# A list scheduler's rough clock gets other durations: a four-layer residual kernel on one core

## The chip, the core and the metric

The kernel runs on one core of a Trainium2 chip. Its time is device microseconds (us) of one execution. Five engines take part: TensorE (PE, with its weight loads listed as PEld), VectorE (DVE), ScalarE (ACT), GpSimd (POOL) and SyncE (SP), which issues most DMAs. Each engine runs its own instructions strictly in the order in which the program holds them and waits at semaphores for the others.

## The reference

`x` is [8, 512, 256], `cond` is [8, 256]. Four layers follow one another, each added to its input: `x = x + layer(x, cond)`.

```python
# L0: tanh RNN          h_t = tanh(x_t Wx + b + h_{t-1} Wh)
# L1: LSTM              i,f,o,g = split(x_t Wx + b + h_{t-1} Wh);  c_t = f c + i g;  h_t = o tanh(c_t)
# L2: hyperbolic transformer block (maps logmap0/expmap0 around each product), modulated by cond @ w_ada
xm = expmap0(layer_norm(logmap0(x)) * (1 + sc_msa) + sh_msa)
q, k, v = (to_heads(plin(xm, w, b)) for w, b in ...)          # 16 heads of 16
attn = softmax(logmap0(q) logmap0(k)^T / 4) logmap0(v)
x1 = mobius_add(x, expmap0(g_msa * logmap0(plin(from_heads(expmap0(attn)), w_o, b_o))))
ff = plin(plin(modulated(x1), w_f1, b_f1), w_f2, b_f2)        # 256 -> 1024 -> 256
out = mobius_add(x1, expmap0(g_mlp * logmap0(ff)))
# L3: mixture of experts, 4 experts of 256 -> 1024 -> 256 and a shared one
gate = softmax((means(x) @ gate_w + gate_b) * (1 + scale) + shift);  top 2, renormalised
out = sum_e w[b, e] * mask[e] * (gelu(x ew1 + eb1) ew2 + eb2) + gelu(x sw1 + sb1) sw2 + sb2
```

## The kernel before

The first half of the span (to about 1250 us) is the two recurrences with the products that feed them. The second half is the function `transformer_and_experts`, which computes the block (L2) and the experts (L3) for the eight batch elements b = 0 to 7, 512 tokens each.

**Pieces and streams.** The second half is written as Python generators, each of which emits instructions and yields where another may go on. They are put into nine streams:

- Stream 0 is the main one, which keeps TensorE full: attention(0), attention(1), attention(2), then experts(b-3) and attention(b) in turn for b = 3 to 7, and last experts(5), experts(6), experts(7). Call "a period" one experts(b-3) with the attention(b) that follows it.
- Streams 1 to 4 carry batch element b from its attention to its experts: `last_sums` and `drain` (1), `close` (2), `feed_forward` (3), `end` (4). In data order: `end` divides the attention sums (tiles `ov`, `o`), transposes (`p_oT`), multiplies with w_o (`pao`, `ao`), adds the residual (`ra_...`) and modulates (`mf_...`); `feed_forward` transposes (`p_mT`) and multiplies (`pf`, `f`, `f2`); `close` adds the second residual (`rf_...`), transposes the result into `xT` (`pyT`), makes the gate (`gs`, `pg`) and the experts' input `xf`, a copy of `xT` rounded for TensorE.
- Streams 6 to 8 prepare the heads of later elements (`heads_inputs`, `heads`: tiles `q`, `k`, `v`, `scales_...`, transposes `q_p`, `k_p`, copies `q_t`, `k_t`) and transpose and store finished elements (`pout`). Streams 3 to 7 can be held back for a while (`HELD`).

In an attention each slot has a score product `sc` (64x128 by 64x512), ACT's exponential `ex` out of it, and the product `po` of `ex` with `v`; there are 64 `ex` of 128x512 in each of eight attentions. In the experts each slot has six products `ph` from `xf` and a weight tile `we`, ACT's gelu `g`, a split into two parts that TensorE's fast format takes (ACT's copy `h`, DVE's difference `h<-g,h`), six products `py`, and, at the end of each expert, DVE's weighted sum of `py` into `xT`. Only three experts are run for an element: the shared one (i = 4) and the two chosen (i = 0 and 1), eight slots each, so that `ph_b_i_m` is slot m of expert i of element b; `ph_b_4_0` is the first and `ph_b_1_7` the last. The `py` of a slot stand three slots behind its `ph`.

**What sets the order.** While the program is built, every instruction of the second half goes through a wrapper `Timed`, one for each engine. It issues the instruction (so the profile's line for all of them is L2101) and adds it to a `Clock`, which models when each engine would be free: an instruction starts when its engine is free and its inputs are ready, and lasts `Timed.cost`. `Clock.AFTER[e][f]` is the delay from the end of a writer on engine e to the start of a reader on f. Costs are polynomials in the size: TensorE's by passes, and for the others a constant and a part for each element. `interleave` then chooses, piece by piece, which stream goes on: among those that are `due` before the modelled time at which TensorE is free, the one of lowest rank (streams 1 to 4 are 0, heads 2, the main stream 3, late stores 4), and if none is due the one that is due first. Streams 5 to 8 also stand back while VectorE or ScalarE is booked more than `clock.backlog` beyond TensorE. So the model's durations decide only the order in which instructions are written into each engine's queue.

**Tables.** ACT needs a function table: `gelu` and `tanh` share one, `exp` and `tanh` another, `exp` and `ln` a third. `Timed.table` follows which one is loaded in the order as it is written. Loads show as ACT_TABLE_LOAD, in L2098 where the kernel asks for one ahead and in L2101 where the function itself brings it.

Of the kernel before, what the change touches and what calls it, by code (L numbers as in the profile page):

```python
# [14 lines left out]
ALU = mybir.AluOpType  # L15
# [4 lines left out]
B, T, D = 8, 512, 256  # L20
# [216 lines left out]
class Front:  # L237
# [55 lines left out]
    def task(self, engine, name, needs, cost, fn, bank=None):  # L293

        self.groups[0][engine].append((name, needs, cost, fn, bank))
# [5 lines left out]
    def any(self):  # L301
        return any(any(g.values()) for g in self.groups)
# [4 lines left out]
    def run(self, engine, step, room=0.0):  # L307

        by, end = {"PE": (1.0, 2.3), "ACT": (2.0, 2.8), "DVE": (0.2, 1.0)}[engine]
        by, end = step * self.STEP + by, step * self.STEP + end  # L310
        first = True
        while True:
            for g in self.groups:
                if not g[engine]:
                    continue
                name, needs, cost, fn, bank = g[engine][0]
                at = self.ready(needs)
                if at is None or at > by or not (first or engine == "PE" and cost <= room):
                    continue
                if bank is not None and bank not in self.held:  # L320
                    free = [i for i, t in enumerate(self.free) if t is not None and t <= by]
                    if not free:
                        continue
                    self.held[bank] = min(free, key=lambda i: self.free[i])
                    self.free[self.held[bank]] = None
                break
            else:
                return
            g[engine].pop(0)
            fn()  # L330
            self.done[name] = end
            if engine in ("ACT", "DVE") and name in self.held:
                self.free[self.held[name]] = end
            room, first = room - cost, False
# [1674 lines left out]
class Clock:  # L2009
# [1 line left out]


    AFTER = {
        "V": {"V": 0.12, "S": 0.13, "M": 0.2, "G": 0.15, "D": 0.15}, "S": {"V": 0.15, "S": 0.1, "M": 0.28, "G": 0.18, "D": 0.15},
        "M": {"V": 0.2, "S": 0.2, "M": 0.0, "G": 0.2, "D": 0.2}, "G": {"V": 0.06, "S": 0.1, "M": 0.15, "G": 0.1, "D": 0.15},
        "D": {"V": 0.1, "S": 0.1, "M": 0.1, "G": 0.1, "D": 0.1},
    }
# [68 lines left out]
class Timed:  # L2086
# [33 lines left out]
    def cost(self, op, outs, ins, args, kw):  # L2120
        n, late = math.prod(outs[-1].shape[1:]), 0.0
        if self.name in "VG":
            n = max(math.prod(t.shape[1:]) for t in (*outs, *ins))
        if self.name == "M":
            if op == "transpose":
                passes = 1 if outs[0].dtype == F32R else 2
            else:
                passes = 1 if kw["lhsT"].dtype == F32R or outs[0].shape[0] == 32 else 4
            cost = max(0.03, n * passes / 2400) + 0.003
        elif self.name == "D":  # L2130
            cost, late = 0.06 + n * P * 4 / 360e3, 2.0
        elif self.name == "G":
            cost = 0.3 + n * 0.165 if ALU.pow in args else 0.1 + n * (0.0022 if op == "tensor_tensor" else 0.0034)
        elif self.name == "S":
            cost = 0.05 + n * 0.00083 + (0.09 if len(outs) > 1 or hasattr(kw.get("bias"), "tensor") else 0.0)
        else:
            fast = op in ("tensor_copy", "tensor_scalar") and ins[0].space == outs[0].space
            by_token = any(t.shape[1:] == (1,) or list(t.shape[1:]) == [1] for t in ins)
            cost = 0.07 + n * (0.00052 if fast else 0.00104) + 0.06 * by_token + 0.13 * (len(outs) > 1)
        return cost, outs, ins, late  # L2140


# [97 lines left out]
```

## Time and profile before

| | before |
|---|---|
| median of three runs | 2471.36 us (2469.95 to 2475.51) |
| profiled execution, its own time | 2467.43 us |
| span of the profile | 2465.6 us |
| mean granted TensorE clock | 0.95 |
| PE busy | 2088.8 us, 85% |
| DVE busy | 1797.7 us, 73% |
| ACT busy | 1487.3 us, 60% |
| POOL busy | 398.9 us, 16% |

The profile is one execution. Times in it are microseconds from the start of the span; "mean ns" is the mean duration of one instruction as recorded, from its start to its recorded end, so that consecutive instructions of one engine can overlap in the records. Idle time before a group is followed by what released it. In tables by windows, each engine has its busy time and its instructions; then come the granted clock (1.00 is full), the share of DMA engines in use and GB/s. Some 1.8 us of the time lie outside the span. A difference of 0.2% is about 5 us.

Landmarks of the second half: attention(0) 1308 to 1355, attention(1) 1358 to 1420, attention(2) 1426 to 1508, a transition 1508 to 1546, the first `ph` at 1546.40. The first period ends at about 1670 and the next four at 1807, 1943, 2080 and 2208; experts(5), (6) and (7) follow.

### The profile page before, as it was taken

The page shows a single profiled execution, that of the slowest core. Times are in us where ns is not written, and L with a number is a line of the kernel's source. Part 1 is how long each engine was busy: PE and PEld are TensorE (multiplying, and loading weights), DVE is VectorE, ACT ScalarE, POOL GpSimd, SP SyncE. Part 2 cuts the span into 40 slices and gives each one's busy share as a digit, 9 for nine tenths or more (in the row PEclk, how much of TensorE's full clock was granted, in tenths as well). Part 3 has the DMA queues.
Part 4 walks back from the last instruction along what each step waited for, and adds up shares of the span by engine and source line. Part 5 has one row for each costly group of instructions (what it writes and reads, how often), then busy time and mean ns, then how long its engine had stood idle before and what let it go on. Part 6 is the DMA issues. An engine that isn't in the chain of part 4 may idle for free.

```text
span 2465.6 us, 89629 instructions
## 1 busy us (share of the span) xinstructions
PE 2088.8 (85%) x36885; PEld 1480.7 (60%) x36885; DVE 1797.7 (73%) x7672; ACT 1487.3 (60%) x4847; POOL 398.9 (16%) x615
## 2 busy tenths in 40 slices
PE   6779876788877899988838986899898999999799
PEld 5566655666656666666524432657566574757587
DVE  5777777788888787887843658766878777777763
ACT  3556566655666666666528864466575857674344
POOL 2010103010030201002004212203223230301100
PEclk9999999999999999999958776999999999999899
DMA  5111131121312002110160000443435252425364
GB/s 153 54 46 49 42 97 42 50 64 60 95 53 66 26 23 55 28 28 20 39 197 24 22 29 24 150 141 132 164 112 167 82 177 81 158 88 173 120 221 146
DMA packets 129458, 215.52 MB, mean 87 GB/s; under 512 B 50356, under 2 KB 85799, under 8 KB 129040
## 3 DMA queue, kind: packets, MB, share of 16 engines
q1 hardware_dynamic: 117528, 170.06, 21.6%
q0 software_dynamic: 10432, 37.11, 4.7%
q8 instruction: 289, 4.73, 0.8%
q10 hardware_dynamic: 1088, 2.62, 0.3%
q14 instruction: 121, 0.99, 0.1%
HBM read 158.82 MB, written 50.92 MB: 85 GB/s over the span
## 4 chain that ended last, share of the span: by engine, by line
PE 64%; DVE 23%; ACT 6%; issue 4%; DMA 1%; POOL 1%; SPq 0%; DVEq 0%; POOLq 0%; ACTq 0%
PE pL L903 25%; PE ph L2101 7%; PE py L2101 7%; PE po L2101 6%; PE sc L2101 6%; DVE turned L1000 4%; DVE scan_out L1004 3%; ACT th L967 3%; PE pX L574 3%; DVE slots_h L1020 2%; PE pf L2101 2%; PE pR L903 2%; DVE h L2101 2%; DVE scan_in L1014 1%; PE pao L2101 1%
## 5 line engine op out<-in xcount | busy, mean ns | idle before, releaser
L903 PE MATMUL pL<-wh,slots_h 128*8 128x128 f32 (+1 forms) x16384 | 554.6, 275 | 202.9 <-DVE slots_h L1020 200.1
L903 PEld LDWEIGHTS pL<-wh,slots_h 128*8 128x8 f32 (+1 forms) x16384 | 374.4, 99 | 376.9 <-DVE slots_h L1020 335.9
L1000 DVE STREAM_TRANSPOSE turned<-pL 128x128 f32<-128x128 f32 x1024 | 324.0, 316 | 158.6 <-PE pL L903 91.3
L967 ACT ACTIVATE scan_in<-turned 128x32 f32<-128x32 f32 x1024 | 266.0, 260 | 284.8 <-DVE turned L1000 278.3
L2101 PE MATMUL py<-h,we 128*128 128x512 f32 x1152 | 306.5, 401 | 19.9 <-DVE xT L2101 14.8
L2101 ACT ACTIVATE ex<-sc 128x512 f32<-128x512 f32 x512 | 268.2, 617 | 86.2 <-PE sc L2101 84.1
L2101 PE MATMUL ph<-xf,we 128*128 128x512 f32 x1152 | 304.3, 398 | 0.0
L2101 PEld LDWEIGHTS py<-h,we 128*128 128x128 f32 x1152 | 214.4, 191 | 70.3 <-issue 18.6
L2101 PEld LDWEIGHTS ph<-xf,we 128*128 128x128 f32 x1152 | 214.5, 190 | 48.9 <-issue 5.6
L967 ACT ACTIVATE th<-scan_out 128x8 f32<-128x8 f32 x1024 | 214.6, 215 | 47.5 <-DVE scan_out L1004 4.8
L1004 DVE TENSOR_TENSOR_SCAN scan_out<-scan_in 128x32 f32<-128x32 f32 x1024 | 220.4, 225 | 17.7
L903 PE MATMUL pR<-r_L_cond_Wh,slots_h 128*8 128x64 f32 (+3 forms) x8192 | 213.7, 221 | 13.9 <-ACT slots_h L967 13.2
L1020 DVE SCALAR_TENSOR_TENSOR slots_h<-scan_in,th 128x8 f32<-128x8 f32 x1024 | 171.8, 168 | 58.8 <-ACT th L967 1.7
L2101 DVE TENSOR_TENSOR h<-g,h 128x512 fp32r<-128x512 f32 x192 | 138.7, 726 | 87.4 <-ACT h L2101 86.5
L967 ACT ACTIVATE slots_h<-r 128x16 f32<-128x16 f32 x512 | 110.1, 215 | 145.0 <-DVE r L974 140.0
L2101 PE MATMUL sc<-q_t,k_t 64*128 64x512 f32 x512 | 175.3, 510 | 18.9 <-ACT ex L2101 17.6
L903 PEld LDWEIGHTS pR<-r_L_cond_Wh,slots_h 128*8 128x8 f32 (+3 forms) x8192 | 170.2, 101 | 17.9 <-ACT slots_h L967 16.0
L2101 PEld LDWEIGHTS sc<-q_t,k_t 64*128 64x128 f32 x512 | 75.4, 203 | 160.3 <-ACT ex L2101 126.6
L903 PE MATMUL pL<-wx,XL 128*32 128x128 f32 x4096 | 161.1, 275 | 0.0
L2101 PE MATMUL po<-ex,v 128*32 128x512 f32 x1024 | 157.2, 669 | 0.0
L2101 ACT ACTIVATE g<-ph,b 128x512 f32<-128x512 f32 x128 | 88.2, 689 | 104.6 <-PE ph L2101 98.7
L974 DVE STREAM_TRANSPOSE r<-pR 128x64 f32<-128x64 f32 x512 | 123.8, 242 | 6.7 <-PE pR L903 6.7
(469 smaller groups left out, 3105.4 us busy)
## 6 DMA issues: line engine op xcount, KB each, us to landing
we<-sde SPq DMA_DIRECT2D x128, 512.0 KB
we<-sd SPq DMA_DIRECT2D x64, 512.0 KB
sde<-parts POOLq DMA_DIRECT2D x32, 512.0 KB, 3.6
raw<-in_L_cond_ew POOLq DMA_DIRECT2D x32, 256.0 KB, 4.6
sd<-parts POOLq DMA_DIRECT2D x8, 512.0 KB, 3.1
xd<-XT SPq DMA_DIRECT2D x4, 1024.0 KB
q<-qd SPq DMA_DIRECT2D x8, 512.0 KB
wl_o<-sd_o SPq DMA_DIRECT2D x8, 512.0 KB
```

The lines of the kernel that those rows point to most:

```text
L574: self.nc.tensor.matmul(bank[:, :D], lhsT=self.u[at][:, c, :], rhs=self.w[n][:, c, :], start=c == 0, stop=c == DC - 1)
L903: nc.tensor.matmul(out[32 * j : 32 * j + m], lhsT=lhsT, rhs=rhs_of(j), start=start, stop=stop, skip_group_check=True)
L967: i = tanhs[what, t] = nc.scalar.activation(out, x, AF.Tanh, scale=scale)
L974: V.transpose(flat(r), flat(pR[q % 2]))
L1000: V.transpose(flat(o), pre[piece])
L1004: V.tensor_tensor_scan(sc[:, c].rearrange("p b s -> p (b s)"), dd[:, 2 + 2 * c].rearrange("p b s -> p (b s)"), dd[:, 3 + 2 * c].rearrange( ...
L1014: V.scalar_tensor_tensor(dd[:, 2:6:2, :, 3], dd[:, 0:2, :, 2], 1.0, sc_old[:, :, :, 3], ALU.add, ALU.mult)
L1020: V.scalar_tensor_tensor(out[:, c], dd[:, 6 + c, :, 2], 1.0, th[c], ALU.add, ALU.mult)
L2101: r = f(*args, **kw)
```

## The change

Six lines of the model alone. In `Clock.AFTER` the delay between two instructions of VectorE falls from 0.12 to 0.02 and between two of ScalarE from 0.1 to 0.03. In `Timed.cost` GpSimd's power operation goes from 0.3 + 0.165 n to 0.65 + 0.148 n; ScalarE's constant goes from 0.05 to 0.19; VectorE's constant goes from 0.07 to 0.18, and its fast operations from 0.00052 to 0.00068 for each element. No instruction's operands change.

```diff
     AFTER = {
-        "V": {"V": 0.12, "S": 0.13, "M": 0.2, "G": 0.15, "D": 0.15}, "S": {"V": 0.15, "S": 0.1, "M": 0.28, "G": 0.18, "D": 0.15},
+        "V": {"V": 0.02, "S": 0.13, "M": 0.2, "G": 0.15, "D": 0.15}, "S": {"V": 0.15, "S": 0.03, "M": 0.28, "G": 0.18, "D": 0.15},
...
         elif self.name == "G":
-            cost = 0.3 + n * 0.165 if ALU.pow in args else 0.1 + n * (0.0022 if op == "tensor_tensor" else 0.0034)
+            cost = 0.65 + n * 0.148 if ALU.pow in args else 0.1 + n * (0.0022 if op == "tensor_tensor" else 0.0034)
         elif self.name == "S":
-            cost = 0.05 + n * 0.00083 + (0.09 if len(outs) > 1 or hasattr(kw.get("bias"), "tensor") else 0.0)
+            cost = 0.19 + n * 0.00083 + (0.09 if len(outs) > 1 or hasattr(kw.get("bias"), "tensor") else 0.0)
         else:
...
-            cost = 0.07 + n * (0.00052 if fast else 0.00104) + 0.06 * by_token + 0.13 * (len(outs) > 1)
+            cost = 0.18 + n * (0.00068 if fast else 0.00104) + 0.06 * by_token + 0.13 * (len(outs) > 1)
```

## The prediction

> **What bounds the kernel now.** I read the page's busy times and chain first, to see which engine sets the end, then the second half by windows, then single queues where TensorE sat idle. The change reorders the second half alone; up to about 1250 us nothing moves.
>
> ```profile
> PE 2088.8 (85%) x36885; PEld 1480.7 (60%) x36885; DVE 1797.7 (73%) x7672; ACT 1487.3 (60%) x4847; POOL 398.9 (16%) x615
> ...
> PE 64%; DVE 23%; ACT 6%; issue 4%; DMA 1%; POOL 1%; SPq 0%; DVEq 0%; POOLq 0%; ACTq 0%
> ```
>
> TensorE carries the chain, so a better order can only recover TensorE's idle time and its lowered clock. How much there is, by windows (busy by PE, PEld, DVE, ACT, POOL; granted clock; DMA): the transition, the second period, the last attention's period without next heads, the stretch before experts(6).
>
> ```profile
> 1508.00:1546.00 38.00, 13.39 (x75) 10.37 (x72) 35.55 (x127) 14.42 (x40) 15.35 (x18) 0.58 0.06 22
> 1670.00:1807.00 137.00, 128.89 (x650) 84.72 (x646) 104.72 (x337) 90.23 (x192) 33.90 (x30) 0.96 0.38 133
> 2080.00:2208.00 128.00, 123.81 (x646) 82.46 (x644) 93.79 (x325) 88.94 (x185) 26.71 (x27) 1.00 0.38 126
> 2272.00:2320.00 48.00, 31.30 (x118) 23.08 (x117) 42.47 (x183) 13.72 (x27) 6.74 (x6) 0.79 0.42 137
> ```
>
> A full period leaves 137.00 - 128.89 = 8.1 us of TensorE idle; the same subtraction gives 8.2 and 8.3 in the next two and 4.2 in the last. The two long idle stretches, 24.6 us in 1508 to 1546 and 16.7 us in 2272 to 2320, are VectorE's (35.55 of 38, 42.47 of 48). Where the 8.1 us lie, in TensorE's queue (start, duration, idle before and releaser):
>
> ```profile
> 1739.62 0.54 PE L2101 MATMUL q_p<-ident_r,q_s 128*128 128x128 f32 x4 [1.23 <-POOL q_s L2101]
> ...
> 1746.47 1.58 PE L2101 MATMUL py<-h,we 128*128 128x512 f32 x3 [2.79 <-DVE xT L2101]
> ...
> 1771.13 0.90 PE L2101 MATMUL pout<-ident,xT 128*128 128x128 f32 x3 [1.44 <-DVE xT L2101]
> ```
>
> The first two, with 0.29 more, are the stall in the experts (4.3 us): VectorE is behind, because the side streams' operations were put in a few slots. The third, with three waits of `sc` (0.37, 0.69, 0.46), is the attention's start (3.0 us); 0.85 lie in a wait for `h`.
>
> In the middle of an attention ACT is the limit:
>
> ```profile
> 1761.20 0.58 ACT L2101 CAST q_t<-q_p 128x512 fp32r<-128x512 f32 x1
> 1761.80 1.28 ACT L2098 ACT_TABLE_LOAD   x1
> 1763.09 1.09 ACT L2101 ACTIVATE ex<-sc 128x512 f32<-128x512 f32 x2
> ...
> 1787.06 10.20 ACT L2101 ACTIVATE ex<-sc 128x512 f32<-128x512 f32 x20
> ```
>
> **What the change moves.** Set beside each other, the two programs have the same instruction counts on PE, DVE, POOL and SP, and the same DMAs; ACT has eight more table loads, 26 for 18. The model gets VectorE and ScalarE slower, so side work is due later and spreads. POOL's and SP's queues only change places with it (`q_p`, `k_p` inputs, `xr`, `ssr`, stores); I cost that at nothing while POOL is busy 33.90 of 137 us. If that cover goes, the price is the 1.23 us wait for POOL's `q_s` once more in each of four periods, 5 us.
>
> *Is the new clock truer?* The row says: 20 `ex` in 10.20 us, 0.51 each, while the page's mean of one is 617 ns; the records overlap. The old cost of an `ex` is 0.05 + 0.425 = 0.475, the new one 0.615. So the new figures hit the recorded duration and not the spacing. The Trainium skill's "Perfetto Trace Analysis", section "Optimizing Scalar/DVE Operations", speaks against the change in the same sense: it says that a profiled latency is about twice the engine's overhead, as the second half overlaps the next instruction. By that the engines are now booked too heavily and the order should get worse; the row agrees about the overlap, but what the order does must be read from the order.
>
> *The stall in the experts (gain).* In slots `ph_1_0_4` to `ph_1_1_6` I summed VectorE's operations between successive splits `h`, with the spacing of each kind in the trace (h 608 ns, xT 304, a 128x256 squared sum 350 + 116, dependent 128x4 196). Before: one slot holds 14.19 us of TensorE work (it took all four `pf` and a `pao`), and later ones 4.73 and 3.46 us of VectorE work against 3.10 of TensorE. After: the TensorE work is 3.83, 6.83, 6.83, 4.92, 4.92, and then 2.74 a slot, and VectorE's 1.97, 1.73, 1.73, 2.63, 4.17, 1.26, 4.19, 1.96, 2.19. A slot over 2.74 is followed by lighter ones, and the three-slot lag of `py` absorbs it. I book the whole 4.3 us and 0.7 of lowered clock (12 us from 1736 at 0.94): 5.0 in each of three periods, **-15.0**; bounds 0 and -15, plus the 4.2 idle of the last period, which I leave.
>
> *The transition and experts(0).* `ph_0_4_0` stands ahead of `p_oT` of element 2, which waited 4.48 us for VectorE's `o`; VectorE's work from the last `ov` to the last `xf` of element 1 falls from 31.3 to 29.7 us. Between 1.6 and 4.5, I take **-3.0**. In experts(0), 1580 to 1600, TensorE is idle 2.5 us at clock 0.91 for the same reason as above: **-3.0**, bounds 0 and -4.
>
> *Table loads (loss).* `rf_sy`, a tanh in `close`, stood in the experts, where gelu's table holds tanh. After, it stands after the ln/exp load in attentions 4 to 7 (behind `sc` of 4_0_2_2, 5_0_3_3, 6_0_0_1, 7_0_2_3), so that each gets a load for the tanh and one back. Eight loads of 1283 ns are 10.3 us if all lie on the path, 0 if in ACT's idle time at the attention's start (2.44, 3.04, 1.02 us before the `ex` at 1772, 1776, 1779). The first lies near that start, the second beside back-to-back `ex`: one and a half loads each, 1.93 x 4 = **+7.7**. The skill's "ScalarE: Activation LUTs", section "What ACT_TABLE_LOAD costs", counts a drain of 1380 ns with each load, 2.66 us in all, so that eight would be 21.3. The rows above show no drain: the cast ends at 1761.78, the load starts at 1761.80, and `ex` starts 1.29 us later. I go by the rows.
>
> *Later side work in attentions (loss).* What moves out of the experts lands in the next attention: `pyT` and `pg` of element 2 stand about one of the four groups later. VectorE's work from the last split of experts(b-1) to the last `xf` of b, which experts(b) needs, goes from 33.2 to 41.8, 51.5 and 43.5 us for b = 2, 3, 4, from 23.7 to 45.4 for b = 5, and from 23.5 to 32.9 for b = 6. TensorE's own work there is 43.3 after. The excess is 0, 8.2, 0.2 and 2.1: 10.5 at most; 0 at least, since before the same stretch lasted 51.2 us, and VectorE's queue would just fit. Nearer the lower end: **+4.3**.
>
> *The end.* Before experts(6), where VectorE is the bound, 9.4 us more work stand behind the last split (32.9 - 23.5), of which 6.8 come from slots ahead of it that now run lighter: **+2.6**, bounds 0 and 9.4. Ahead of `ph_7_4_0` the same is **+0.9**.
>
> *Attentions 1 and 2* (1358 to 1508) run half cold: 1400 to 1450 has clock 0.61 with TensorE busy 44.89 of 50. Side pieces stand 16 to 30 instructions earlier. A shift of 5% of these 150 us either way is 7.5; no row says which way, so I take 0 and keep it for the range.
>
> Sum: -15.0 - 3.0 - 3.0 + 7.7 + 4.3 + 2.6 + 0.9 = **-5.5 us**. The profiled execution took 2467.43 (span 2465.6 and 1.8 around it), so about 2462; it is 3.9 under the median of 2471.36, and from the median I say 2466.
>
> **Rivals.**
>
> *More of it: about 2454.* If the loads fall in ACT's idle time and the later side work is hidden, only -21 + 3.5 = -17.5 remain. For it: ACT idles 6.5 us at each attention's start. Against: the second load stands where ACT has no gap over 0.5 us.
>
> *Slower: the attentions pay, about 2479.* The late `rf` chain and its two loads hold up ACT and TensorE, whose clock then falls, as in 1768 to 1780 (0.72, TensorE busy 10.10 of 12). Such a disturbance once more costs 2.57 of loads, 1.9 idle and about 1.9 of clock (12 us at 0.72, part of it idle): 6.4 in each of attentions 4 to 7, 25.6. With 3.5 of the end, and 21 gained, the sum is +8.1. It decides where an attention loses over (21 - 3.5) / 4 = 4.4 us. For it: every attention after the first change has more VectorE work, none less. Against: the last `ex` are tight only in ACT, and TensorE has other work there.
>
> *The clock is no truer: about 2471.* The bookings overstate both engines alike, the relative order of pieces hardly matters, and what leaves the experts comes back in the attentions, -21 + 21.
>
> **How the numbers follow.** The forecast, 2460 to 2471, has 0.36, of which 0.24 is faster by over 0.2% (about 5 us, what a measurement of this kernel can tell from no change) and 0.12 within it. The larger gain has 0.20, all faster. The third has 0.10: 0.06 the same, 0.04 slower. The slower rival, 2474 to 2492, has 0.34: 0.02 the same and 0.32 slower. That gives 0.44, 0.20 and 0.36. Range 2446 to 2488: the gain's end with all of the transition's bound and some of the clock, and the rival with the 7.5 of the cold attentions; about 0.05 lies below and 0.13 above.
>
> **What would show it.** Right: no wait of `py` for `xT` over 1 us in the experts of 0 to 3, 26 table loads, periods of about 135 us, TensorE idle in a period 5 to 6 us. If the slower rival holds, idle time and lowered clock stand at `pyT`, `pg` or `sc` in attentions 4 to 7 and the periods are over 137 us. If the table loads are hidden, `sc` waits for `ex` no more than before. The prediction is wrong outright if attentions 0 to 2, which I set at zero, carry the difference.

## The result, and the profile after

The changed kernel takes 2481.20 us (median of 20 runs, 2472.91 to 2489.30) against 2475.60 us (20 runs, 2468.39 to 2479.07): a ratio of 1.0023, 95% interval 1.0013 to 1.0033, so about 5.7 us slower. The forecast was 5.5 us faster; the time lies inside the range of 2446 to 2488. The profiled execution took 2484.90 us, with a span of 2483.0 us. That is 17.5 us over the profiled execution of before, three times the difference of the medians, so stages are compared with second profiles beside them.

The busy times and the chain of the changed kernel:

```profile
PE 2098.7 (85%) x36885; PEld 1485.3 (60%) x36885; DVE 1783.7 (72%) x7672; ACT 1495.8 (60%) x4855; POOL 391.7 (16%) x615
...
PE 67%; DVE 20%; ACT 7%; issue 4%; DMA 1%; POOL 1%; SPq 0%; DVEq 0%; POOLq 0%
```

VectorE's share of the chain fell from 23% to 20% and TensorE's rose from 64% to 67%, as a better fed TensorE would show, and yet the span is longer. ACT has eight instructions more, the loads. The windows say where it went. I cut them at the first and last gelu of an element's experts, so that they are experts(1), attention(4), experts(2), attention(5). First before, then after (columns as in the prediction):

```profile
1674.41:1759.95 85.54, 80.39 (x395) 64.30 (x394) 66.50 (x173) 51.33 (x111) 30.88 (x27) 0.98 0.49 170
1759.95:1811.28 51.33, 48.37 (x254) 20.42 (x253) 38.13 (x162) 38.76 (x79) 3.02 (x3) 0.93 0.21 71
1811.28:1896.68 85.40, 80.28 (x395) 64.20 (x394) 66.33 (x173) 51.32 (x111) 31.44 (x27) 0.98 0.52 171
1896.68:1947.93 51.25, 48.20 (x254) 20.43 (x253) 38.21 (x163) 38.76 (x79) 3.02 (x3) 0.93 0.21 71
```

```profile
1688.14:1766.42 78.28, 76.99 (x379) 61.95 (x378) 53.69 (x141) 49.42 (x106) 25.51 (x24) 1.00 0.53 184
1766.42:1823.85 57.43, 52.40 (x270) 22.51 (x269) 45.81 (x194) 43.61 (x86) 5.97 (x6) 0.91 0.20 66
1823.85:1901.53 77.68, 77.68 (x387) 63.20 (x386) 50.85 (x128) 49.36 (x106) 27.18 (x24) 1.00 0.54 190
1901.53:1964.67 63.14, 53.37 (x266) 22.38 (x265) 51.67 (x219) 43.40 (x88) 5.99 (x6) 0.88 0.17 55
```

The experts run as forecast: TensorE has no idle time left in experts(2) (77.68 of 77.68 us) and the clock is 1.00 for 0.98. But VectorE is busy 12.8 and 15.5 us less in the two experts and 7.7 and 13.5 us more in the attentions that follow, which take 6.1 and 11.9 us more at a lower clock (0.91 and 0.88 for 0.93). TensorE's idle time moves with it: over four such pairs it falls from 17.4 to 3.6 us in the experts, and rises from 11.3 to 21.6 us in attentions 4 to 7.

All stages, from the starts of the first and last `ex` and `g` in the traces; "again" is the second profile of the same kernel, in the experiments below:

| us | before | again | after | again |
|---|---|---|---|---|
| start to first ex | 1307.3 | 1311.4 | 1313.0 | 1310.5 |
| attentions 0 to 2 | 199.1 | 200.1 | 209.4 | 199.5 |
| last ex to first g of experts(0), and experts(0) | 122.2 | 122.2 | 117.6 | 119.6 |
| attention(3) | 45.9 | 45.9 | 48.2 | 48.2 |
| experts(1) to (4) | 337.0 | 338.7 | 314.1 | 313.9 |
| attentions 4 to 7 | 201.4 | 200.1 | 227.1 | 228.0 |
| experts(5) to the end | 252.8 | 252.8 | 253.6 | 253.5 |

The first two rows vary by themselves: the first, whose order is the same in both kernels but for a few instructions just before the first `ex`, differs by up to 5.7 us between executions, and attentions 0 to 2 of the changed kernel by 9.9. The four rows from attention(3) on repeat within 1 us in sum: 837.1 and 837.5 us before, 843.0 and 843.6 after, 6 us more. That is the size of the difference of the medians.

### The profile page after: what moved, and what is told of

Read it like the earlier page. It is cut to its first block, busy times and chain, and to the rows that moved or that the text cites. A ratio compares the mean times of both kernels' runs of the same rounds, so it can differ in the third digit from the quotient of the medians.

```text
span 2483.0 us, 89628 instructions
## 1 busy us (share of the span) xinstructions
PE 2098.7 (85%) x36885; PEld 1485.3 (60%) x36885; DVE 1783.7 (72%) x7672; ACT 1495.8 (60%) x4855; POOL 391.7 (16%) x615
## 4 chain that ended last, share of the span: by engine, by line
PE 67%; DVE 20%; ACT 7%; issue 4%; DMA 1%; POOL 1%; SPq 0%; DVEq 0%; POOLq 0%
PE pL L903 25%; PE ph L2101 10%; PE py L2101 9%; PE sc L2101 5%; PE po L2101 5%; DVE turned L1000 4%; DVE scan_out L1004 3%; ACT th L967 3%; PE pX L574 3%; DVE slots_h L1020 2%; PE pf L2101 2%; PE pR L903 2%; DVE scan_in L1014 1%; ACT ex L2101 1%; PE pao L2101 1%
## 5 line engine op out<-in xcount | busy, mean ns | idle before, releaser
L903 PE MATMUL pL<-wh,slots_h 128*8 128x128 f32 (+1 forms) x16384 | 556.3, 276 | 204.7 <-DVE slots_h L1020 202.1
L2101 PE MATMUL py<-h,we 128*128 128x512 f32 x1152 | 299.0, 394 | 3.9 <-DVE xT L2101 3.9
L2101 PE MATMUL sc<-q_t,k_t 64*128 64x512 f32 x512 | 179.1, 514 | 23.4 <-ACT ex L2101 20.6
```

The source lines that it names most:

```text
L903: nc.tensor.matmul(out[32 * j : 32 * j + m], lhsT=lhsT, rhs=rhs_of(j), start=start, stop=stop, skip_group_check=True)
L2101: r = f(*args, **kw)
```

## The experiments

Three theories were open. L: the eight table loads are the loss of attentions 4 to 7. C: VectorE's late chain (residual, `pyT`, gate) is. H: the order of attentions 0 to 2, which I had set at zero, carries the difference.

**no_reload.** In the changed order, the tanh of elements 2 to 5 is issued as an exp, so that this kernel leaves the tanh out, while the clock goes on counting a tanh.

```diff
...
+            if need == "tanh" and self.clock.real == ("exp", "ln") and args[0].tensor.name[:5] in ("rf_2_", "rf_3_", "rf_4_", "rf_5_"):
+                given = (*args[:2], AF.Exp, *args[3:])
+            elif need and need not in self.clock.real:
+                self.clock.real = TABLES[need]
+            r = f(*given, **kw)
```

> Exactly the order of the changed kernel, but the tanh `rf_sy` of elements 2 to 5 is issued as an exp (so the tanh itself is left out), and the eight extra table loads go with it: 18 loads for 26. Theory L (the loads are the loss of the attentions): about 10 us under the changed kernel, that is 4 to 5 us under before (ratio to before 0.998), and attentions 4 to 7 (last g of an element's experts to the first g of the next) each 2.6 us shorter than in the changed kernel. Theory C (the late residual, pyT and gate chain on VectorE is the loss): at most 3 us under the changed kernel, ratio to before 1.001 to 1.002; attentions 4 to 7 shorten by under 1 us each. Theory H (attentions 1 and 2 carry the difference): as theory C here, since nothing is changed there.

Measured: ratio 1.0029 (1.0014 to 1.0045), no faster than the changed kernel; attentions 4 to 7 together 226.6 us, for 227.1 and 228.0. Groups of table loads in the stretch of these attentions, of the changed kernel and then of this one (count, busy, mean ns, idle before):

```profile
L2098 ACT ACT_TABLE_LOAD x8 | 10.3, 1283 | 0.1
L2101 ACT ACT_TABLE_LOAD x8 | 10.3, 1283 | 0.1
```

```profile
L2099 ACT ACT_TABLE_LOAD x4 | 5.1, 1283 | 0.1
L2109 ACT ACT_TABLE_LOAD x4 | 5.1, 1283 | 0.1
```

10.3 us of ACT are gone and the attentions keep their length. ACT's queue shows why, in the changed kernel and here:

```profile
1784.65 1.28 ACT L2101 ACT_TABLE_LOAD   x1
1785.94 0.20 ACT L2101 ACTIVATE rf_sy<-rf_n 128x4 f32<-128x4 f32 x1
1786.05 1.06 ACT L2101 ACTIVATE ex<-sc 128x512 f32<-128x512 f32 x2
1787.78 1.09 ACT L2101 ACTIVATE ex<-sc 128x512 f32<-128x512 f32 x2 [0.66 <-PE sc L2101]
```

```profile
1780.54 0.23 ACT L2109 ACTIVATE rf_sy<-rf_n 128x4 f32<-128x4 f32 x1
1781.63 1.08 ACT L2109 ACTIVATE ex<-sc 128x512 f32<-128x512 f32 x2 [0.87 <-PE sc L2109]
1783.82 1.09 ACT L2109 ACTIVATE ex<-sc 128x512 f32<-128x512 f32 x2 [1.11 <-PE sc L2109]
```

Where the load stood, ACT now waits for scores. Theory L falls: it asked for a ratio of 0.998 and for 2.6 us less in each of these attentions. Even between the far ends of the two intervals of the times, 1.0033 and 1.0014, lie less than 5 us, not 10. Theories C and H had these attentions shorter by under 1 us each, as they are.

**early_tanh.** The changed kernel, with the attention held until the tanh is issued.

```diff
+            yield "done", ("tanh", name)      # in close, behind the tanh
...
             if b >= AHEAD:
+                yield "need", ("tanh", f"rf_{b - 2}")
                 S.preload_act_table_set("natural_log_exp_and_others")
```

> The changed kernel with one more condition: attention(b) for b from 3 starts only when the close of element b-2 has issued its tanh, so that it stands ahead of the exp/ln table load. Up to attention(4) the order is that of the changed kernel; table loads are 18. Theory L: as without the loads, about 10 us under the changed kernel (ratio to before 0.998), since the loads are gone. Theory C: more than that, 10 to 18 us under the changed kernel (ratio 0.995 to 0.998), since the chain to the gate also ends earlier, or, if holding back attention(b) leaves TensorE idle at its end of the experts, nothing is gained: each wait there takes the place of what is won. Theory H: the loss of attentions 1 and 2 stays, some 5 to 10 us over before less whatever is won in attentions 4 to 7.

Measured: ratio 1.0058 (1.0039 to 1.0077), 14 us over before. The loads are gone, and in attention(4) the first `ex` comes 18.6 us after the last `g`, for 6.1. Over attentions 4 to 7 this start takes 46.7 us more than in the changed kernel, and the rest 43.7 less: the wait took the place of what was won, and more. The half of theory C that I put after "or" happened, and worse than "nothing is gained".

**head_new and tail_new.** The new durations before, or from, experts(0).

```diff
     def times(self, new):
+        self.new = new
+        self.AFTER = {e: dict(d) for e, d in Clock.AFTER.items()}
+        if new:
+            self.AFTER["V"]["V"], self.AFTER["S"]["S"] = 0.02, 0.03
...
             yield "need", ("close", b)
+            clock.times(False)        # tail_new: True, and the reverse at the start
```

> The new durations only until experts(0) begins (so attentions 0 to 2 are in the changed kernel's order), the old ones from there. Theory H (the order of attentions 0 to 2 is the loss): 6 to 10 us over before, ratio 1.002 to 1.004, and the stretch from the first ex of attention(0) to the last ex of attention(2) is 209 us as in the changed kernel's profile, not 199. Theories L and C: the same as before within 3 us (ratio 0.999 to 1.001), and that stretch varies between profiles by itself.

> The opposite: the old durations until experts(0) begins, the new ones from there, with the 26 table loads. Theory H: 2 to 5 us under before (ratio 0.998 to 0.999), since the rest of the changed kernel is no loss. Theories L and C: as slow as the changed kernel, 4 to 8 us over before (ratio 1.002 to 1.003); attentions 4 to 7 together about 25 us longer than before, the experts 1 to 4 about 20 us shorter.

Measured: head_new 1.0017 (1.0002 to 1.0032), tail_new 0.9993 (0.9979 to 1.0007). So the version with the new durations in the head alone is about 4 us slower than before, and the one with them in the rest alone can't be told from it. In tail_new attentions 4 to 7 take 223.9 us, 22.5 more than before, and experts 1 to 4 take 22.2 less. The times have the signs of theory H, but both lie just outside the ranges that I gave it, and head_new's attentions 0 to 2 took 204.7 us and not 209.

The stages don't bear theory H out. Six profiles of this study have the changed order up to the first `g` of experts(0), and eight have that of before. Their attentions 0 to 2 average 205.5 us (199.5 to 210.2) and 201.3 (199.1 to 203.1), 4 us more with the new order. But the transition behind them averages 42.8 and 47.0 us, so that both reach the first `g` 248.3 us after the first `ex`. And experts(0) takes 80.9 us in head_new and 71.3 in tail_new, for 76.0 in before and 75.7 in the changed kernel: there each of the two versions has an order that neither kernel has. So they don't split the changed kernel's loss in two, and head_new's 4 us may well be those of its own experts(0).

**before_again and after_again.** Both kernels unchanged.

> The kernel before, unchanged, for a second profile. What varies by itself: the recurrences (1307.3 us to the first ex) by some us. Theory H (the order of attentions 0 to 2 costs the changed kernel about 5 us): first ex of attention(0) to last ex of attention(2) within 199 to 203 us; experts 1 to 4 and attentions 4 to 7 within 1 us of the first profile. If it comes out at 204 or more, theory H has no ground.

> The changed kernel, unchanged, for a second profile. Theory H: the stretch of attentions 0 to 2 within 204 to 210 us (209.4 in the first); attentions 4 to 7 together 225 to 229 us.

Measured: the columns "again" above. The stages behind the last `ex` of attention(2) repeat within 2 us; after_again's attentions 0 to 2, at 199.5, are a miss of what I expected, as are before_again's experts 1 to 4 and attentions 4 to 7, which I gave 1 us and which moved by 1.7 and 1.3. What the changed order costs in attentions 0 to 2 is an average over executions, not a fixed cost.

**head_hold.** What costs in the head? In the changed kernel TensorE waits at the start of attention(2) for an `ex` that stands in ACT's queue behind `ohc`, and `ohc` waits for VectorE, which does element 0's `mf_uu` ahead of the last `ov`. From VectorE's queue, ACT's and TensorE's:

```profile
1432.51 2.26 DVE L2101 TENSOR_SCALAR mf_uu<-ra_o,mf_r,mf_sh 128x256 f32<-128x256 f32 x4
1434.70 0.68 DVE L2101 COPY ov<-po 128x512 f32<-128x512 f32 x1
```

```profile
1438.48 0.55 ACT L2101 ACTIVATE ohc<-ohc 128x64 f32<-128x64 f32 x2 [4.36 <-DVE ohc L2101]
```

```profile
1442.55 1.28 PE L2101 MATMUL sc<-q_t,k_t 64*128 64x512 f32 x2 [5.16 <-ACT ex L2101]
```

```diff
+            if name == "mf_0":
+                yield "need", ("attention", 1)
             u = unit([P, NT, D], f"{name}_uu")
```

> The changed kernel with one hold: the scaled residual `mf_0_uu` of element 0 is not begun before attention(1) has ended, so that VectorE copies attention(1)'s last `ov` ahead of it. Theory D (in the changed kernel VectorE's early `mf_0_uu` delays `ov`, that delays the last sums `ohc` for which ACT waits with the exponentials of attention(2) behind it, and TensorE waits 5.16 us): that wait falls to 1 to 2.5 us, attentions 1 and 2 together are 3 to 6 us shorter, ratio to before 1.0000 to 1.0012. Theory N (attentions 1 and 2 differ by the half clock alone, wherever the idle time falls): the wait shrinks but the time doesn't, ratio 1.002 to 1.003.

Measured: TensorE's wait falls to 3.28 us (I had said 1 to 2.5), and from the last `ex` of attention(1) to the first of attention(2) it takes 8.9 us for 13.1 (9.0 before), but the ratio is 1.0024 (1.0008 to 1.0040):

```profile
1443.05 0.79 PE L2103 MATMUL sc<-q_t,k_t 64*128 64x512 f32 x1 [3.28 <-ACT ex L2103]
```

The 4.2 us won there don't show in the time; against the first profile of the changed kernel 3.6 of them came back in the transition (45.5 us for 41.9, last `ex` to first `g`), against the second 1.6. Theory D is right that the wait falls and wrong about the time, which came out as theory N has it.

**v_only, s_only, g_only.** One engine's numbers at a time.

```diff
-            cost = 0.07 + n * (0.00052 if fast else 0.00104) + ...
+            cost = 0.18 + n * (0.00068 if fast else 0.00104) + ...     # v_only, with V after V 0.02
-            cost = 0.05 + n * 0.00083 + ...
+            cost = 0.19 + n * 0.00083 + ...                            # s_only, with S after S 0.03
-            cost = 0.3 + n * 0.165 if ALU.pow in args else ...
+            cost = 0.65 + n * 0.148 if ALU.pow in args else ...        # g_only
```

> Of the change only VectorE's two numbers and its delay after itself. In attentions 1 and 2 VectorE's order is nearly that of before (nothing of `mf_0_uu` ahead of attention(1)'s last `ov`), and there are 20 table loads. Theory D: no loss there, ratio 0.998 to 1.001, with a small gain in the experts. If the loss of the changed kernel were of the later stages: 1.001 to 1.003.

> Of the change only ScalarE's constant and its delay after itself. All eight `mf_0_uu` stand ahead of attention(1)'s last `ov` (two more than in the changed kernel before the next sums), table loads are 18 as in before. Theory D: the loss of attentions 1 and 2 is all there, 4 to 8 us, ratio 1.0015 to 1.0035. If the loss needs both engines' numbers: 0.999 to 1.001.

> Of the change only GpSimd's power operation. The order moves least: ten small pieces of `mf_0` stand ahead of attention(1)'s last sums, but `mf_0_uu` behind them; 18 table loads. Theory D: 0 to 2 us of loss, ratio 1.0000 to 1.0010. Any ratio over 1.002 would speak against it.

Measured: 1.0027 (1.0012 to 1.0042), 1.0041 (1.0028 to 1.0055), 1.0066 (1.0042 to 1.0090). GpSimd's part alone is slower than all together, ScalarE's probably too, and VectorE's can't be told from the whole; the parts' losses add up to 1.3%, the whole costs 0.23%. s_only has the long attentions 0 to 2 that I expected (210.5 us) and a ratio a little over what I gave it, but its transition is 9.3 us shorter than that of before, so that little of the loss stands in the head. What I expected of v_only and g_only was wrong. v_only's attentions 0 to 2 take 210.4 us although nothing of `mf_0_uu` stands ahead of the last `ov`: theory D doesn't explain these. g_only, whose order I called the least moved, lost the most, outside the head: its `pyT` stands at the start of the attention, ahead of its input, and each of attentions 4 to 6 takes 4.1 to 4.6 us more.

```profile
1780.46 0.47 PE L2101 MATMUL pyT<-ident,rf_o 128*128 128x128 f32 x1 [3.64 <-DVE rf_o L2101]
```

**tail_ahead.** tail_new, with the gate for the heads moved from 2 to 6 us.

```diff
-                clock.backlog = 2.0
+                clock.backlog = 6.0
```

> Old durations until experts(0), the new ones from there, and from attention(2) on the heads stand back only when VectorE or ScalarE is booked 6 us beyond TensorE, not 2. The last q and k transposes of the next element then stand in the experts again (slots 1_0 to 1_2, not behind the last ph). Theory S (the new durations close this gate too early, and the transposes between the last ph and the first sc hold up each attention's start): from the last g to the first ex 3.1 us again (4.5 to 6.1 in the changed kernel), 6 to 10 us less in all, ratio to before 0.995 to 0.998. Theory M (they are only moved, what leaves the attentions comes back in the experts): ratio 0.998 to 1.001, as without that change (0.9993).

Measured: 0.9990 (0.9975 to 1.0004). Attentions 4 to 7 fall from 223.9 to 204.4 us and experts 1 to 4 rise from 314.8 to 332.0: theory M, moved and not saved. The 48 transposes that the changed kernel has at the starts are back in the experts, but the start of attentions 4 to 6 did not fall to 3.1 us; it stands at 6.4. There ACT has two loads, and the first `ex` stands behind `rf_sy`, which waits 0.64 us for VectorE's `rf_n`. The loads alone are not what holds it: ahead_exp below has one of the two, its `rf_sy` waits 1.92 us, and the start is again 6.4.

**att_new.** The new durations inside attentions 3 to 7 alone.

```diff
             clock.attending = True
+            if b >= AHEAD:
+                clock.times(True)      # and False where the experts begin
```

> The new durations only inside attentions 3 to 7; attentions 0 to 2 and all experts by the old ones. Table loads are 18, the transposes and rf_sy stand where before has them; only pyT and pg of the element two before come one to three sc later. Theory P (the later pyT and gate alone cost the attentions): each of attentions 4 to 7 0.5 to 2 us longer than before, ratio 1.001 to 1.003. Theory W (what costs is that work of VectorE is carried from the experts into the attention, which doesn't happen here): ratio 0.999 to 1.001, attentions within 0.5 us.

Measured: 1.0046 (1.0029 to 1.0063). Attentions 4 and 5 take 5.6 and 3.1 us more, 6 and 7 nothing. Theory P in sign, with a larger loss than I gave it and another distribution: one to three scores' difference in the place of `pyT` and the gate goes with 5.6 us, or with none.

**less_vector and before_less.** Where the 25 us of attentions 4 to 7 lie. Both keep their kernel's order to the instruction and leave out VectorE's in-place steps of elements 2 to 7, so they don't compute the layer.

```diff
+LEFT_OUT = tuple(f"{n}_{b}" + end for b in range(2, 8) for n, end in (("mf", "_uu"), ("ao", ""), ("f2", "")))
...
+            if not (self.name == "V" and at in again and at.startswith(LEFT_OUT)):
+                r = f(*args, **kw)
```

> Exactly the order of the changed kernel, but for elements 2 to 7 VectorE's in-place steps on the modulated input, the attention output and the feed-forward output (scale, shift, gate, clip factors) are left out: 22 instructions for each element, some 10 us of VectorE. Theory V (attentions 4 to 7 wait for VectorE's late chain): attentions 4 to 7 together at most 212 us (227 in the changed kernel), experts(5) to experts(6) shorter too, 15 us or more under the changed kernel, ratio to before 0.995 or less. Theory O (the order on TensorE and ACT itself, with its table loads and transposes): attentions 4 to 7 over 220 us, ratio 1.000 to 1.002.

> Exactly the order of the kernel before, with the same 22 VectorE instructions of elements 2 to 7 left out as in the changed kernel's order (there: ratio to before 0.9928, attentions 4 to 7 together 210.0 us for 227 to 228). Theory V (the changed order makes the attentions wait for VectorE, the order of before doesn't): attentions 4 to 7 fall by less than 6 us from 201 (the start's waits for xT stay), the experts lose part of their 4.3 us stall, and the two versions end within 6 us of each other: ratio 0.990 to 0.995. Theory U (VectorE's work counts alike in any order): attentions 4 to 7 fall by 12 us or more, and the ratio is 0.990 or less, as far below before as the other was below the changed kernel (0.9905).

Measured: 0.9928 (0.9908 to 0.9949) in the changed order and 0.9901 (0.9884 to 0.9918) in the order of before. less_vector came out as theory V had it (at most 212 us and 0.995), not as theory O. But over the whole kernel the steps are worth the same in both orders, 1% of the time (0.9928 / 1.0023 = 0.9905), as theory U has it. In attentions 4 to 7 they are not: 227.1 falls to 210.0 (17.1), 201.4 to 192.1 (9.3), between the bounds that I gave theories V and U. Attention(4) and (5) in the changed order, lightened:

```profile
1770.27:1821.67 51.40, 49.18 (x270) 21.57 (x269) 41.00 (x182) 43.39 (x86) 5.74 (x6) 1.00 0.21 70
1898.56:1957.52 58.96, 51.62 (x269) 22.24 (x268) 47.13 (x210) 43.30 (x87) 5.77 (x6) 0.91 0.21 66
```

Attention(4) is back at before's 51.3 us, attention(5) is not. Cut each attention in three, and add up the four:

| us over before, attentions 4 to 7 | after | less_vector against before_less |
|---|---|---|
| last g to first ex | +10.1 | +9.9 |
| first ex to last ex | +7.9 | +0.1 |
| last ex to first g | +7.7 | +8.0 |

The second profiles of both kernels give +10.1, +9.9 and +7.9. The middle is VectorE's chain: with less of its work the two orders are equal there, in the sum of the four. In the changed kernel the chain stops TensorE in attention(4) at a `sc` behind 18 `py`, and in attention(5) at `pyT`; before has 0.4 and nothing at these places, and less_vector has no wait at the first and 0.68 us at the second:

```profile
1778.03 0.46 PE L2101 MATMUL sc<-q_t,k_t 64*128 64x512 f32 x1 [2.46 <-DVE xT L2101]
...
1929.59 0.47 PE L2101 MATMUL pyT<-ident,rf_o 128*128 128x128 f32 x1 [1.12 <-DVE rf_o L2101]
```

The start and the end are the same without these 22 instructions for each element. They are order, by the rows; no run takes away one of them alone. At the starts stand 48 transposes that before did in the experts (16, 12, 12 and 8). At the ends of attentions 5 and 7, which take 8.6 and 5.9 us for 3.4, a `pot` stands behind the last `po` and ahead of the first `ph`; attentions 4 and 6, where none stands there, end in 3.3 us. In the changed kernel and lightened alike, at attention(5):

```profile
1959.59 0.66 PE L2101 MATMUL pot<-ident,ov 128*128 128x128 f32 x4 [1.78 <-DVE ov L2101]
...
1963.17 4.29 PE L2101 MATMUL ph<-xf,we 128*128 128x512 f32 x10 [2.23 <-DVE xf L2101]
```

```profile
1952.24 0.66 PE L2108 MATMUL pot<-ident,ov 128*128 128x128 f32 x4 [1.79 <-DVE ov L2108]
...
1955.83 2.50 PE L2108 MATMUL ph<-xf,we 128*128 128x512 f32 x5 [2.24 <-DVE xf L2108]
```

**ahead_exp and ahead_exp_end.** An attempt to beat both kernels: tail_ahead without its extra loads (ahead_exp), and the same with the old durations again from experts(5) (ahead_exp_end).

```diff
+                S.activation(sy, n, AF.Exp, scale=2.0)
+                V.tensor_scalar(sy, sy, 1.0, None, ALU.add)
+                V.reciprocal(sy, sy)
+                V.tensor_scalar(sy, sy, -2.0, 1.0, ALU.mult, ALU.add)
...
+            clock.times(b < 5)        # ahead_exp_end alone
```

> The version with old durations up to experts(0), the new ones from there and heads ahead (ratio 0.9990), and the tanh of elements 2 to 5 computed as 1 - 2 / (exp(2n) + 1), with three more small VectorE operations: 18 table loads for 26. In that version ACT runs back to back through the whole attention (first to 16th ex 9.1 us, 16th to last 33.3). Theory A (there the loads are on the path): attentions 4 to 7 each about 2.5 us shorter, 10 us in all, ratio 0.994 to 0.996. Theory B (something else ends the attention, the late chain): attentions as before, ratio 0.998 to 1.000.

> The same, with the old durations again from experts(5) on, where the new ones cost 4 us after the last attention (252.8 to 256.8 us from the first g of experts(5) to the end). Theory A: ratio 0.992 to 0.995. Theory B: 0.997 to 0.999. If the end depends on what stands before it, no difference to the last.

Measured: 1.0009 (0.9996 to 1.0021) and 1.0006 (0.9988 to 1.0024). Both are slower than either theory had it, and attentions 4 to 7 are longer than with the loads (208.8 us for 204.4), with three more VectorE operations in the chain. Theory A rested on a misreading of tail_ahead: ACT does not run back to back there. The later of the two extra loads is followed by a wait for VectorE that covers it:

```profile
1783.34 1.28 ACT L2106 ACT_TABLE_LOAD   x1
1787.68 0.20 ACT L2109 ACTIVATE mf_u<-mf_c 128x4 f32<-128x4 f32 x1 [3.06 <-DVE mf_c L2109]
```

No version that computes the whole layer is shown to beat before; tail_ahead and tail_new come nearest, at 0.9990 and 0.9993, and both intervals hold 1.

## Why the prediction was wrong, step by step

The sign was wrong: -5.5 us forecast, +5.7 measured. By terms, "measured" from both pairs of profiles, the first two rows from the six and eight profiles named above:

| step | forecast | measured |
|---|---|---|
| attentions 0 to 2 | 0 | about +4 |
| transition | -3.0 | about -4 |
| experts(0) | -3.0 | -0.3 |
| attention(3) | not in the sum | +2.3, +2.4 |
| experts(1) to (4) | -15.0 | -22.8, -24.8, work moved out included |
| table loads | +7.7 | 0.5 to 1.3 |
| the rest of attentions 4 to 7 | +4.3 | +24 to +27, work moved in included |
| experts(5) to the end | +3.5 | +0.8, +0.6 |

**The stall in the experts** was right. TensorE's idle time in experts(1) to (4) falls from 17.4 to 3.6 us, some 12 of it in the three periods for which I had booked 15 with the clock; what the experts win beyond that went to the attentions with the transposes. In experts(0) the idle time falls too, from 4.3 to 2.8 us at clock 1.00 for 0.98, but with the changed order 26 more matmuls stand there, 350 for 324, and the 3.0 us that I booked don't show.

**The later side work in attentions** is the step that failed, by size: +4.3 forecast, +24 to +27 measured. Taken together, experts(1) to (4) and attentions 4 to 7 with their loads were to win 3.0 us, and lost 2.8 and 3.1. I compared sums over the whole stretch: VectorE's 41.8 to 51.5 us of work against TensorE's 43.3, and let the excess alone cost. A sum doesn't see where in the stretch a piece stands. VectorE's chain cost 7.9 us in the middle, 3.2 of it in attention(4), for which I had no excess at all, and 4.4 in attention(5), the one with an excess of 8.2. The ends of attentions 5 and 7, where `pot` stands ahead of the first `ph`, cost 7.7 us with VectorE's full load and 8.0 with less of it. The transposes that now stand between the last `ph` and the first `sc` I had only as a change of places in POOL's queue, and costed at nothing on TensorE and ACT; the starts, where they stand, take 10.1 us more, partly for work that the experts no longer do. How much of the 10.1 is a loss, no run shows.

**The table loads** failed too, the other way. I took the middle of an attention for ACT-bound, from 20 `ex` back to back. A row of before spoke against it: there TensorE is busy all the time by the profile, and ACT is not.

```profile
1779.00:1807.00 28.00, 28.00 (x167) 10.11 (x170) 19.54 (x91) 26.09 (x58) 1.01 (x1) 1.00 0.10 38
```

In the changed order ACT waits there, so that loads hide. By the figure of the Trainium skill's page "ScalarE: Activation LUTs", section "What ACT_TABLE_LOAD costs", 2.66 us for each switch, the estimate for the eight was 21.3 us. In no_reload attentions 4 to 7 are 0.5 to 1.3 us shorter without them.

**Attentions 0 to 2** I took at zero for want of a row and kept at 7.5 us either way for the range. They are 4 us longer on average, and the transition behind them 4 us shorter, so that up to experts(0) nothing was won of the 3.0 us that I had booked for the transition. The scatter from 199.5 to 210.2 us of one and the same order goes with the granted clock, which changes in steps. The 6 us that repeat in both pairs stand from attention(3) on: 2.3 and 2.4 there, 2.8 and 3.1 in experts(1) to (4) and attentions 4 to 7, 0.8 and 0.6 behind these. One thing stays open: tail_new, whose ACT and GpSimd have the same order from attention(3) on, takes 837.2 us there in its one profile, as before does. Its attention(3), in which VectorE's side pieces stand otherwise, has nothing of the 2.4; why its attentions 4 to 7 are 3 to 4 us shorter than the changed kernel's, no run shows.

**The rivals.** The time is nearest to "slower, about 2479", whose price of 6.4 us for each of attentions 4 to 7 (25.6 in all) is near the 25.7 and 27.9 measured. That is partly luck, since 10.3 of the 25.6 are table loads, which cost next to nothing. Its mechanism is half right: the late chain and its clock, without the loads; and the gain against it was larger than booked, so that this rival alone would have ended near zero. "The clock is no truer", that what leaves the experts comes back in the attentions, describes the second half best: -22.8 and +25.7. I gave it 0.10.

**The marks that I named.** 26 loads came, and experts(1) and (2) without a wait of `py` for `xT` over 1 us; in experts(0) and (3) such a wait of 1.6 and 1.1 us is left. The periods I said would be 135 us are 135.7, 140.8, 133.1 and 131.6 (136.9, 136.7, 136.6 and 128.2 before), so that only one is over the 137 that I named for the slower rival. TensorE's idle time in a period, which I put at 5 to 6 us, is 6.3, 9.8, 5.1 and 3.9.

## What to carry to other kernels

Work that is moved out of a stall is not gone: ask for the stage that receives it which instruction of an in-order queue will now stand ahead of its input, and give that place a price, since sums of work over a stretch don't see it. A model's constants don't add up one by one; here each engine's corrected numbers alone cost 0.3 to 0.7%, and all together 0.2%, and the one threshold that was set anew beside them (tail_ahead) gave no gain that can be told from zero. When a run is to split a change in two, check at the seam that each half has an order of one of the kernels; here experts(0) had neither, and in head_new took 5 us more than in either.

## What the runs showed of the hardware

The granted clock is 0.50 or 1.00 in these traces and moves in steps of about 3.4 us. In the changed kernel's attention(1) it is 0.50 for 20.5 us after a wait of TensorE of 2.35 us, and in its second profile for 6.8 us at the same place. Over attentions 0 to 2 it averages 0.78 and 0.82 in these two profiles of one instruction stream, which takes 209.4 and 199.5 us there. A table load takes 1283 ns and ACT goes on at once behind it; 16 of them in attentions 4 to 7 (20.6 us) could be halved without an effect on the time that could be measured.
